# Layer 3's weight tiles taken by twos, in a four-layer graph network on one core

## The chip, the cores and the metric

The kernel runs on one core of one Trainium2 chip. The metric is the time on the device in microseconds, from start to end of one execution. The kernel before took 2709.49 us (median of three runs, 2709.22 to 2711.38).

## The reference, cut to what matters

There are 16 graphs of 1024 nodes with 256 features each, and an adjacency matrix of 1024 x 1024 whole numbers (0 or 1) for each. Four layers follow each other, each a layer norm, a relu and a graph layer that is added to x: two attention layers of one head, a layer of mean messages, and an attention layer of four heads with 64 features a head. The fourth is the one that is changed:

```python
h = einsum('bnd,hde->bhne', nodes_embed, W)            # H = 4 heads, 64 features each
weight = mask * (e_src[:, :, :, None] + e_dst[:, :, None, :])
weight = leaky_relu(weight, negative_slope=0.01)
weight = where(node_adj[:, None] == 0, NEG, weight)
attention = softmax(weight, axis=-1)
dst = einsum('bhij,bhje->bhie', attention, h) + bias
out = relu(dst) + h                                    # then a norm over each head's 64 features
```

(The reference sums over five kinds of edges; with an adjacency of zeros and ones only the first is there.)

## The kernel before

Each graph is a Python generator that records instructions, and each `yield` says by how many units the graph moves on in a list. The recorder always takes the graph with the lowest position, so the yields decide how the instructions of neighbouring graphs are mixed. Graphs start 120 units apart, and one is some 260 long: two or three are under way at a time. A scheduler then sets the final order on each engine; what is marked `later` keeps its place.

Layer 3 makes the unnormalised attention of one head in tiles `p` of 128 source nodes x 1024 target nodes on VectorE, and multiplies each tile at once on TensorE. A product takes 64 target nodes as its stationary side (`part`), so two of them, `c` = 0 and 1, use two halves of the array's columns. The outcome has 65 columns, 64 features and the sum for the softmax. Eight outcomes share one PSUM tile, `pss[g]`, four for each g. `start` is set on the first write to a PSUM tile alone.

```python
def layer3(b, xs, mask, norm, res):
    ...                                    # projection, exponentials, hb: features times exp, and exp
    yield 8
    for h in range(H):
        next_row = everywhere(d_row[h + 1], "row3") if h + 1 < H else None
        pss = [hd_ps.tile([P, HALF], F32, tag="hd", name="ps_o3") for _ in range(NHALF)]
        for j in range(NT):
            p = work.tile([P, N], F32, tag="p3", name="p3", bufs=3)
            nc.vector.scalar_tensor_tensor(p, row, q[:, j, h : h + 1], mask[:, j, :], op0=OP.max, op1=OP.mult)   # L887
            for i in range(NT):
                g, k = divmod(i, PER)
                for c in range(2):
                    part = slice(c * P // 2, (c + 1) * P // 2)
                    nc.tensor.matmul(                                                                            # L893
                        pss[g][part, k * HW : (k + 1) * HW], p[:, i * P : (i + 1) * P][:, part], hbv[:, j, h, :],
                        start=(j == 0 and k == 0), stop=(j == NT - 1 and k == PER - 1), skip_group_check=True,
                    )
            yield 1.4
        for g in range(NHALF):             # read out: L901, L902
            o = pss[g][:, : PER * HW].rearrange("p (k e) -> p k e", e=HW)
            rz = small.tile([P, PER], F32, tag="rz", name="rz")
            nc.vector.reciprocal(rz, o[:, :, HO])
            nc.vector.tensor_tensor(res[:, g * PER : (g + 1) * PER, h, :], o[:, :, :HO], ..., op=OP.mult)
        row = next_row
    return hs
```

The `hd` pool has two PSUM tiles, so a head can't begin until the head ahead of it is read out. Layer 1 has the same kind of tile, with products of full width: each of its first two row blocks gets its product as soon as a tile is there, the other six afterwards.

```python
def layer1(b, xs, mask, norm, after):
    ...
    (d_row,) = spread(column(hs[:, :, D + 1 : D + 2], 1), 1, (S - 1.0,), "l1")   # a transpose on TensorE (L672), ...
    row = everywhere(d_row, "row")                                             # ... then out to DRAM and back (DMA)
    yield 5
    for j in range(NT):
        p = weights("p1")                                                      # eight buffers
        nc.vector.scalar_tensor_tensor(p, row, q[:, j : j + 1], mask[:, j, :], op0=OP.max, op1=OP.mult)  # L793
        for i, ps in enumerate(early):
            product(ps, i, j)                                                  # L786, 128 x 257
        yield 1.3
    ...
```

The rest is only named here: projections (L659), transposes (L653), layer 0's products (L730), layer 2's (L844), and `tail`, the last norm of a graph.

Of the kernel before, what the change touches and what calls it, by code (L numbers as in the profile page):

```python
# [8 lines left out]
F32 = mybir.dt.float32  # L9
# [412 lines left out]
def tile_simple_stack(  # L422
# [22 lines left out]
    S, S3 = 0.2, 0.01  # L445
    W3 = D + 2 * H
    HW = HO + 1
    STEP = 1.3
    EARLY = 2

    const = ctx.enter_context(tc.tile_pool(name="const", bufs=1))
# [261 lines left out]
    def layer0(b, xs, m, norm, after):  # L713
        hs = new_hs()
        for n in range(NT):
            ps = project(norm, wx[0], n, D + 2)
            nc.scalar.activation(hs[:, n, : D + 2], ps[:, : D + 2], AF.Copy, scale=norm.rs[n])  # L717
            m.step()
            yield 1.2
        mask = m.bytes  # L720
        row_a, row_b = [everywhere(d, "row") for d in spread(column(hs[:, :, D : D + 1], 1), 1, (1.0, S), "l0")]
        q = small.tile([P, NT], F32, tag="q", name="q")
        nc.scalar.activation(q, hs[:, :, D + 1], AF.Exp, scale=1.0 - S)
        watch(b, 0, hs[:, :, D : D + 2])
        yield 5
        ps_ = []
        early = [at_ps.tile([P, HALF], F32, tag="at", name="ps_o0") for _ in range(EARLY)]

        def product(ps, i, j):
            m = nc.tensor.matmul(  # L730
                ps[:, :D], ps_[j][:, i * P : (i + 1) * P], hs[:, j, :D], start=(j == 0), stop=(j == NT - 1)
            )
            if i < EARLY and j < 7:
                later(m)

        for j in range(NT):
            if m.raws:
                m.step(2)
            p = weights("p0")
            nc.vector.scalar_tensor_tensor(p, row_a, q[:, j : j + 1], row_b, op0=OP.mult, op1=OP.max)  # L740
            z = small.tile([P, 2], F32, tag="z", name="z", bufs=8)
            nc.vector.scalar_tensor_tensor(p, p, 1.0, mask[:, j, :], op0=OP.mult, op1=OP.mult, accum_out=z[:, 0:1])
            nc.vector.reciprocal(z[:, 1:2], z[:, 0:1])
            nc.scalar.activation(hs[:, j, :D], hs[:, j, :D], AF.Copy, scale=z[:, 1:2])  # L744
            ps_.append(p)
            if b == 0:
                gates.append(p)
            for i, ps in enumerate(early):
                if j:
                    product(ps, i, j - 1)  # L750
            yield 2.6
        for i, ps in enumerate(early):
            product(ps, i, NT - 1)
        for i in range(NT):
            if i < EARLY:
                ps = early[i]
            else:
                ps = at_ps.tile([P, HALF], F32, tag="at", name="ps_o0")
                for j in range(NT):
                    product(ps, i, j)  # L760
            e = work.tile([P, D], F32, tag="e", name="e")
            nc.scalar.activation(e, ps[:, :D], AF.Exp)  # L762
            v = work.tile([P, D], F32, tag="v", name="v")
            nc.scalar.copy(v, ps[:, :D])  # L764
            residual(xs, i, v, after, e)
            yield 3.9


    def layer1(b, xs, mask, norm, after):
        hs = new_hs()  # L770
        for n in range(NT):
            ps = project(norm, wx[1], n, D + 2)
            nc.scalar.activation(hs[:, n, : D + 2], ps[:, : D + 2], AF.Copy, scale=norm.rs[n])
            yield 1.4
        (d_row,) = spread(column(hs[:, :, D + 1 : D + 2], 1), 1, (S - 1.0,), "l1")
        row = everywhere(d_row, "row")
        watch(b, 1, hs[:, :, D : D + 2])
        q = small.tile([P, NT], F32, tag="q", name="q")
        nc.scalar.activation(q, hs[:, :, D], AF.Exp, scale=1.0 - S)
        nc.scalar.activation(hs[:, :, D], hs[:, :, D], AF.Exp, scale=S)  # L780
        yield 5
        ps_ = []
        early = [at_ps.tile([P, HALF], F32, tag="at", name="ps_o1") for _ in range(EARLY)]

        def product(ps, i, j):
            nc.tensor.matmul(  # L786
                ps[:, : D + 1], ps_[j][:, i * P : (i + 1) * P], hs[:, j, : D + 1], start=(j == 0), stop=(j == NT - 1)
            )

        for j in range(NT):  # L790
            nc.scalar.activation(hs[:, j, :D], hs[:, j, :D], AF.Copy, scale=hs[:, j, D : D + 1])
            p = weights("p1")
            nc.vector.scalar_tensor_tensor(p, row, q[:, j : j + 1], mask[:, j, :], op0=OP.max, op1=OP.mult)  # L793
            ps_.append(p)
            for i, ps in enumerate(early):
                product(ps, i, j)
            yield 1.3
        for i in range(NT):
            if i < EARLY:
                ps = early[i]  # L800
            else:
                ps = at_ps.tile([P, HALF], F32, tag="at", name="ps_o1")
                for j in range(NT):
                    product(ps, i, j)
            k = b * NT + i
            z = shares[:, k : k + 1]
            nc.vector.reciprocal(z, ps[:, D : D + 1])  # L807
            e = work.tile([P, D], F32, tag="e", name="e")
            nc.scalar.activation(e, ps[:, :D], AF.Exp, scale=z)  # L809
            v = work.tile([P, D], F32, tag="v", name="v")  # L810
            nc.scalar.activation(v, ps[:, :D], AF.Copy, scale=z)
            residual(xs, i, v, after, e)
            yield 3.9


    def layer2(b, xs, norm, after):
# [12 lines left out]
        for n in range(NT):  # L829
            ps = project(norm, wx[2], n, 2 * D)  # L830
            rs = norm.rs[n]
            nc.scalar.activation(hi[:, n, :D], ps[:, :D], AF.Copy, scale=rs)  # L832
            rest = work.tile([P, D], F32, tag="e", name="rest")
            nc.scalar.activation(rest, ps[:, :D], AF.Copy, scale=rs)
            nc.scalar.activation(up[:, n, :D], ps[:, D:], AF.Copy, scale=rs)
            nc.vector.tensor_tensor(lo[:, n, :D], rest, hi[:, n, :D].bitcast(F32), op=OP.subtract)
            nc.vector.tensor_tensor(up[:, n, :D], up[:, n, :D], rows["bias2"], op=OP.add)
            yield 1.1
        for j in range(NT):
            g, jj = divmod(j * P, QUART)  # L840
            ps = hd_ps.tile([P, HALF], F32, tag="hd", name="ps_o2")
# [11 lines left out]
            nc.scalar.copy(edges[:, k : k + 1], ps[:, D : D + 1])  # L853
            nc.vector.tensor_tensor(v, v, up[:, j, :D], op=OP.add)
            residual(xs, j, v, after)
            yield 3.5


    def layer3(b, xs, mask, norm, res):
# [4 lines left out]
        for n in range(NT):  # L864
            ps = project(norm, wx[3], n, W3)
            nc.scalar.activation(hs[:, n, :], ps[:, :W3], AF.Copy, scale=norm.rs[n])
            if n % 2:
# [4 lines left out]
                bias = rows["bias3"].rearrange("p (h e) -> p h e", e=HO).unsqueeze(1).to_broadcast([P, 2, H, HO])  # L872
                nc.vector.tensor_tensor(t, hv, bias, op=OP.add)
                nc.vector.tensor_tensor(t, t, hbv[:, pair, :, HO:].to_broadcast([P, 2, H, HO]), op=OP.mult)
            yield 1.2
        d_row = spread(column(terms[:, :, :H], H), H, (S3 - 1.0,), "l3")
        row = everywhere(d_row[0], "row3")
        watch(b, 2, terms)
        q = small.tile([P, NT, H], F32, tag="q3", name="q3", bufs=2)
        nc.scalar.activation(q, terms[:, :, H:], AF.Exp, scale=1.0 - S3)  # L880
        yield 8
        for h in range(H):
            next_row = everywhere(d_row[h + 1], "row3") if h + 1 < H else None
            pss = [hd_ps.tile([P, HALF], F32, tag="hd", name="ps_o3") for _ in range(NHALF)]
            for j in range(NT):
                p = work.tile([P, N], F32, tag="p3", name="p3", bufs=3)
                nc.vector.scalar_tensor_tensor(p, row, q[:, j, h : h + 1], mask[:, j, :], op0=OP.max, op1=OP.mult)  # L887

                for i in range(NT):
                    g, k = divmod(i, PER)  # L890
                    for c in range(2):
                        part = slice(c * P // 2, (c + 1) * P // 2)
                        nc.tensor.matmul(  # L893
                            pss[g][part, k * HW : (k + 1) * HW], p[:, i * P : (i + 1) * P][:, part], hbv[:, j, h, :],
                            start=(j == 0 and k == 0), stop=(j == NT - 1 and k == PER - 1), skip_group_check=True,
                        )
                yield 1.4
            for g in range(NHALF):
                o = pss[g][:, : PER * HW].rearrange("p (k e) -> p k e", e=HW)
                rz = small.tile([P, PER], F32, tag="rz", name="rz")  # L900
# [48 lines left out]
    def graph(b):  # L949
# [3 lines left out]
        for g in range(NT // 2):  # L953
            norm.pair(xs, g)
            m.step()
            yield 2
        for layer, inputs in ((layer0, (m,)), (layer1, (m.bytes,)), (layer2, ())):
            yield 2
            norm.flip()
            after = Norm()  # L960
            yield from layer(b, xs, *inputs, norm, after)
            norm = after
        yield 2
        norm.flip()
        res = state.tile([P, NT, H, HO], F32, tag="res", name="res", bufs=1)
        hs = yield from layer3(b, xs, m.bytes, norm, res)
# [3 lines left out]

    def loads(b):
        loaded[b] = load_x(b)
        yield 50
        masks[b] = Mask(b)
        yield 0

# [2 lines left out]
    def more():  # L979

        weights01(1, w1, w1_t, a1, (1, 0))
        yield 20
        weights2()
        yield 10
        weights3()
        yield 0

# [1 line left out]
    next(loads_0)  # L989
    weights01(0, w0, w0_t, a0, (0, 1), wait=False)  # L990
    next(loads_0)
    queue = [(33, 0, more())] + [(b * APART, b, graph(b)) for b in range(B)] + [(b * APART - 60, b, loads(b)) for b in range(1, B)]
    while queue:
        queue.sort(key=lambda g: g[:2])
        at, b, g = queue.pop(0)
# [86 lines left out]
```

## Time and profile before

| what | before |
|---|---|
| median of three runs | 2709.49 us |
| span of the profiled run | 2701.4 us |
| instructions | 62281 |
| DMA traffic | 233.73 MB, 87 GB/s on average |
| granted TensorE clock | 0.978 of full speed |

TensorE's products have the name PE in the profile, its weight loads PEld, VectorE is DVE, ScalarE ACT, GpSimd POOL. A float32 product is two instructions each in the profile, so a layer-3 tile, which has 16 products, shows as 32. The page gives each engine's busy time, the span in 40 slices with a digit for the busy tenths, the DMA queues, the chain of work that ended last, and groups of equal instructions. A group's row reads: line, engine, operation, output and inputs, shapes, count, then busy us and mean ns of one, then the idle time just before them and what ended most of it. Matmuls overlap in a pipeline, so the time of one is read from start to start, and not from its duration.

### The profile page before, as it was taken

To read this page: it belongs to the slowest core of one execution; us is meant where nothing else is said; L and a number is where in the kernel's file an instruction comes from. 1 tells how busy PE (TensorE), PEld (TensorE's weight loads), DVE (VectorE), ACT (ScalarE), POOL (GpSimd) and SP (SyncE) were. 2 spreads that over 40 slices of the span, in tenths; PEclk is the share of its full clock that TensorE was granted. 3 is DMA by queue.
4 is the path that set the end of the run, shared out by engine and by line. 5 is a ranking of instruction groups with operands and counts; after the bars stand their busy time and mean duration, and the time that the engine had idled before them with its cause. 6 is when DMAs were issued, how large, how long until landed. Compare 5 with 4: busy or idle time off the path is not lost.

```text
span 2701.4 us, 62281 instructions
## 1 busy us (share of the span) xinstructions
PE 2504.5 (93%) x25682; PEld 2018.0 (75%) x25682; DVE 2021.2 (75%) x4069; ACT 1432.5 (53%) x4065; POOL 418.1 (15%) x390
## 2 busy tenths in 40 slices
PE   5899999999999999999999999999999999999985
PEld 4677787776777778687776877778787777877764
DVE  4357768687686977779677687887778777786868
ACT  4663755627455364654637546374653737546250
POOL 1010212102121030211102111020210202121021
PEclk7899999999999999999999999999999999999998
DMA  4431322424223242331413224242332413224121
GB/s 145 117 83 52 114 72 67 122 64 125 76 69 108 65 120 66 98 80 64 133 53 114 72 64 125 65 133 68 96 82 64 133 52 114 74 63 113 37 63 35
DMA packets 146073, 233.73 MB, mean 87 GB/s; under 512 B 9392, under 2 KB 94512, under 8 KB 145776
## 3 DMA queue, kind: packets, MB, share of 16 engines
q1 hardware_dynamic: 74608, 145.73, 16.7%
q0 software_dynamic: 71168, 83.89, 12.4%
q8 instruction: 205, 3.36, 0.5%
q14 instruction: 92, 0.75, 0.1%
HBM read 212.35 MB, written 17.24 MB: 85 GB/s over the span
## 4 chain that ended last, share of the span: by engine, by line
PE 50%; DMA 13%; issue 13%; DVE 13%; ACT 10%; POOL 1%; SPq 0%; DVEq 0%; POOLq 0%; ACTq 0%
PE ps_o L893 14%; PE ps_o L730 12%; PE ps_proj L659 9%; PE ps_o L786 9%; DMA raw<-in_adj_t 5%; PE ps_o L844 5%; DVE p L887 4%; DMA adj<-in_adj 4%; DMA row<-d_row 3%; PE pt_h L653 2%; ACT hn L631 2%; ACT mask L575 2%; ACT unread L635 1%; DMA d_row<-e_row 1%; DVE p L793 1%
## 5 line engine op out<-in xcount | busy, mean ns | idle before, releaser
L887 DVE SCALAR_TENSOR_TENSOR p<-row,q,mask 128x1024 f32<-128x1024 f32 x512 | 635.3, 1276 | 38.8 <-PE ps_o L893 30.0
L659 PE MATMUL ps_proj<-wx,ht 128*128 128x258 f32 (+2 forms) x2048 | 631.5, 444 | 19.4 <-ACT hs L717 12.8
L893 PEld LDWEIGHTS ps_o<-hb,p 128*64 128x64 f32 x16384 | 513.2, 139 | 126.1 <-issue 72.2
L893 PE MATMUL ps_o<-hb,p 128*64 128x65 f32 x16384 | 563.1, 225 | 16.2 <-DVE p L887 11.1
L786 PE MATMUL ps_o<-hs,p 128*128 128x257 f32 x2048 | 529.7, 398 | 50.0 <-DVE p L793 41.0
L730 PE MATMUL ps_o<-hs,p 128*128 128x256 f32 x2048 | 492.6, 387 | 14.5 <-ACT hs L744 14.0
L659 PEld LDWEIGHTS ps_proj<-wx,ht 128*128 128x128 f32 x2048 | 362.2, 190 | 186.7 <-issue 75.5
L786 PEld LDWEIGHTS ps_o<-hs,p 128*128 128x128 f32 x2048 | 372.1, 193 | 112.6 <-issue 48.5
L730 PEld LDWEIGHTS ps_o<-hs,p 128*128 128x128 f32 x2048 | 383.8, 193 | 70.7 <-ACT hs L744 15.3
L592 POOL TENSOR_SCALAR rs<-mv 128x4 f32<-128x4 f32 (+1 forms) x112 | 56.9, 508 | 1600.3 <-ACT unread L635 1584.7
L631 ACT ACTIVATE hn<-xs,shift 128x256 f32<-128x256 f32 x512 | 236.1, 501 | 115.7 <-DVE shift L627 112.9
L707 DVE SCALAR_TENSOR_TENSOR xs<-e,xs 128x256 f32<-128x256 f32 x256 | 108.2, 423 | 236.8 <-ACT e L762 204.3
L593 POOL TENSOR_TENSOR rs<-rs,neg_half 128x4 f32<-128x4 f32 (+2 forms) x144 | 259.7, 1806 | 10.7
L809 ACT ACTIVATE e<-ps_o,shares 128x256 f32<-128x256 f32 x128 | 59.7, 466 | 349.7 <-DVE shares L807 345.5
L575 ACT ACTIVATE mask<-raw 128x512 uint8<-128x512 int32 x256 | 160.5, 630 | 133.8 <-DMA raw<-in_adj_t 114.7
L844 PE MATMUL ps_o<-hi,adj 128*128 128x258 f32 x1024 | 184.9, 308 | 35.5 <-ACT hi L832 23.7
L653 PE MATMUL pt_h<-ident,hn 128*128 128x128 f32 x1024 | 177.5, 283 | 16.5 <-ACT hn L631 16.2
L635 ACT ACTIVATE unread<-xs,shift 128x256 bf16<-128x256 f32 x384 | 190.7, 497 | 0.6
L844 PEld LDWEIGHTS ps_o<-hi,adj 128*128 128x128 f32 x1024 | 144.3, 192 | 60.7 <-ACT hi L832 29.7
L740 DVE SCALAR_TENSOR_TENSOR p<-row,q 128x1024 f32<-128x1024 f32 x128 | 161.1, 1269 | 30.5 <-DMA row<-d_row 30.5
L654 ACT COPY ht<-pt_h 128x512 f32<-128x512 f32 x256 | 147.2, 588 | 67.3 <-PE pt_h L653 66.8
L708 DVE SCALAR_TENSOR_TENSOR xs<-v,xs 128x256 f32<-128x256 f32 x384 | 161.6, 421 | 26.2 <-ACT v L764 9.7
(101 smaller groups left out, 2644.4 us busy)
## 6 DMA issues: line engine op xcount, KB each, us to landing
raw<-in_adj_t SPq DMA_DIRECT2D x256, 256.0 KB
adj<-in_adj POOLq DMA_DIRECT2D x64, 1024.0 KB, 5.8
row<-d_row SPq DMA_DIRECT2D x112, 512.0 KB
xs<-in_x POOLq DMA_DIRECT2D x32, 512.0 KB, 6.3
out<-res SPq DMA_DIRECT2D x32, 512.0 KB
wx<-in_w SPq DMA_DIRECT2D x3, 256.0 KB
d_row<-e_row SPq DMA_DIRECT2D x48, 4.0 KB
wts<-in_w_t SPq DMA_DIRECT2D x2, 256.0 KB
```

The costliest lines, as they stand in the source:

```text
L575: nc.scalar.activation(self.bytes[:, n, g * HALF : (g + 1) * HALF], raw, AF.Square, accum_out=squares[:, k : k + 1])
L593: nc.gpsimd.tensor_tensor(rs[:, :n], rs[:, :n], neg_half[:, :n], op=OP.pow)
L631: nc.scalar.activation(hn, xs[:, 2 * g + k, :], AF.Relu, bias=shift[:, k : k + 1])
L635: nc.scalar.activation(unread, xs[:, 2 * g + k, :], AF.Square, bias=shift[:, k : k + 1], accum_out=self.var[:, 2 * g + k : 2 * g + k + 1])
L653: nc.tensor.transpose(pt[:, c, k * P : (k + 1) * P], hn[:, c * P : (c + 1) * P], ident)
L659: nc.tensor.matmul(ps[:, :width], norm.ht[:, c, n * P : (n + 1) * P], w[:, c, :width], start=(c == 0), stop=(c == DC - 1))
L708: nc.vector.scalar_tensor_tensor(x, v, 0.0, x, op0=OP.max, op1=OP.add, accum_out=after.sums[:, i % 2 : i % 2 + 1])
L730: m = nc.tensor.matmul(ps[:, :D], ps_[j][:, i * P : (i + 1) * P], hs[:, j, :D], start=(j == 0), stop=(j == NT - 1))
L786: nc.tensor.matmul(ps[:, : D + 1], ps_[j][:, i * P : (i + 1) * P], hs[:, j, : D + 1], start=(j == 0), stop=(j == NT - 1))
L844: nc.tensor.matmul(ps[:, : D + 2], adj_n[g][:, i, jj : jj + P], h[:, i, : D + 2], start=(h is hi and i == 0), stop=(h is lo and i == NT - 1),)
L887: nc.vector.scalar_tensor_tensor(p, row, q[:, j, h : h + 1], mask[:, j, :], op0=OP.max, op1=OP.mult)
L893: nc.tensor.matmul(pss[g][part, k * HW : (k + 1) * HW], p[:, i * P : (i + 1) * P][:, part], hbv[:, j, h, :], start=(j == 0 and k == 0), st ...
```

## The change

Layer 3 makes two tiles first and then multiplies both in one run of 32 products. The run begins with the two first products of the *second* tile, one for each PSUM tile, so that its only wait, for the second tile, stands at its head, and goes on with all of the first tile and the rest of the second. `start` and `stop` move with that order. The aim is that TensorE changes less often between these products and others, and that nothing stops it within a run. Three buffers serve the tiles, as before.

All steps of the list are set anew for it. No other instruction is added or taken away.

```diff
-    STEP = 1.3
+    STEP = 1.6                      # tail
 (layer 0)
-            yield 1.2
+            yield 0.9
-        yield 5
+        yield 4.8
 (layer 1)
-            yield 3.9
+            yield 3.74
 (layer 2)
-            yield 1.1
+            yield 1.14
-            yield 3.5
+            yield 3.22
 (layer 3)
-            yield 1.2
+            yield 1.15
-        yield 8
+        yield 9.44
...
-            for j in range(NT):
-                p = work.tile([P, N], F32, tag="p3", name="p3", bufs=3)
-                nc.vector.scalar_tensor_tensor(p, row, q[:, j, h : h + 1], mask[:, j, :], op0=OP.max, op1=OP.mult)
-
-                for i in range(NT):
+            for j in range(0, NT, 2):
+                ps_ = []
+                for jj in range(j, j + 2):
+                    p = work.tile([P, N], F32, tag="p3", name="p3", bufs=3)
+                    nc.vector.scalar_tensor_tensor(p, row, q[:, jj, h : h + 1], mask[:, jj, :], op0=OP.max, op1=OP.mult)
+                    ps_.append(p)
+
+                runs = [(1, 0), (1, PER)] + [(0, i) for i in range(NT)] + [(1, i) for i in range(NT) if i % PER]
+                for t, i in runs:
                     g, k = divmod(i, PER)
                     for c in range(2):
                         part = slice(c * P // 2, (c + 1) * P // 2)
                         nc.tensor.matmul(
-                            pss[g][part, k * HW : (k + 1) * HW], p[:, i * P : (i + 1) * P][:, part], hbv[:, j, h, :],
-                            start=(j == 0 and k == 0), stop=(j == NT - 1 and k == PER - 1), skip_group_check=True,
+                            pss[g][part, k * HW : (k + 1) * HW], ps_[t][:, i * P : (i + 1) * P][:, part], hbv[:, j + t, h, :],
+                            start=(j == 0 and t == 1 and k == 0), stop=(j == NT - 2 and t == 1 and k == PER - 1),
+                            skip_group_check=True,
                         )
-                yield 1.4
+                yield 2.8
...
 (graph: between layers, before layer 3)
-            yield 2
+            yield 2.36
-        yield 2
+        yield 1.92
 (loads: x first, the first mask tiles later)
-        yield 50
+        yield 30.0
 (more: the weights of layers 1 to 3, for the first graph)
-        yield 20
+        yield 21.6
...
-    queue = [(33, 0, more())] + ... + [(b * APART - 60, b, loads(b)) for b in range(1, B)]
+    queue = [(32, 0, more())] + ... + [(b * APART - 80, b, loads(b)) for b in range(1, B)]
```

With both, x is fetched 80 units ahead of its graph's start (60 before), and the first mask tiles 50 ahead (10 before).

More of the change, by code (lines that the diff above doesn't have):

```diff
@@ L780, in layer1 @@
         nc.scalar.activation(hs[:, :, D], hs[:, :, D], AF.Exp, scale=S)
-        yield 5
+        yield 5.0
         ps_ = []
@@ L955, in graph @@
             m.step()
-            yield 2
+            yield 2.0
         for layer, inputs in ((layer0, (m,)), (layer1, (m.bytes,)), (layer2, ())):
-            yield 2
+            yield 2.36
             norm.flip()
@@ L962, in graph @@
             norm = after
-        yield 2
+        yield 1.92
         norm.flip()
@@ L981, in more @@
         weights01(1, w1, w1_t, a1, (1, 0))
-        yield 20
+        yield 21.6
         weights2()
-        yield 10
+        yield 10.0
         weights3()
@@ L991, in tile_simple_stack @@
     next(loads_0)
-    queue = [(33, 0, more())] + [(b * APART, b, graph(b)) for b in range(B)] + [(b * APART - 60, b, loads(b)) for b in range(1, B)]
+    queue = [(32, 0, more())] + [(b * APART, b, graph(b)) for b in range(B)] + [(b * APART - 80, b, loads(b)) for b in range(1, B)]
     while queue:
```

## The prediction

> **What bounds the kernel now.** I read the page from the top: engine shares, the 40 slices, the chain of waits, the groups.
>
> ```profile
> PE 2504.5 (93%) x25682; PEld 2018.0 (75%) x25682; DVE 2021.2 (75%) x4069; ACT 1432.5 (53%) x4065; POOL 418.1 (15%) x390
> ...
> PE   5899999999999999999999999999999999999985
> ...
> PE 50%; DMA 13%; issue 13%; DVE 13%; ACT 10%; POOL 1%; SPq 0%; DVEq 0%; POOLq 0%; ACTq 0%
> ```
>
> TensorE (PE) is the bound: busy 93% of 2701.4 us, below nine tenths only in the first two and last two slices, and half of the chain that ended last is PE. The idle 197 us divide roughly so: slices of 67.5 us at 5, 8, 8 and 5 tenths give about 34 + 13 + 13 + 34 = 94 us at the ends, so about 100 us in the middle, some 6 us for each of the 16 graphs. Next, the rows of the stage that is changed:
>
> ```profile
> L887 DVE SCALAR_TENSOR_TENSOR p<-row,q,mask 128x1024 f32<-128x1024 f32 x512 | 635.3, 1276 | 38.8 <-PE ps_o L893 30.0
> ...
> L893 PEld LDWEIGHTS ps_o<-hb,p 128*64 128x64 f32 x16384 | 513.2, 139 | 126.1 <-issue 72.2
> L893 PE MATMUL ps_o<-hb,p 128*64 128x65 f32 x16384 | 563.1, 225 | 16.2 <-DVE p L887 11.1
> ```
>
> VectorE (DVE) makes 512 weight tiles of 1.2 to 1.28 us each; TensorE multiplies each by 32 instructions on a 128*64 division of the array. PE waits for them almost nowhere (11.1 us in all), while DVE waits 30.0 us for PE to release a tile: DVE runs ahead as far as three buffers allow. So the case for the change isn't a wait that is printed; it is the switching between 128*64 and 128*128 instructions. Start times of a stretch of the timeline, PE alone, show it:
>
> ```profile
> 1418.09 1.15 PE L893 MATMUL ps_o<-hb,p 128*64 128x65 f32 x32
> 1419.17 0.70 PE L786 MATMUL ps_o<-hs,p 128*128 128x257 f32 x2
> 1419.80 2.09 PE L893 MATMUL ps_o<-hb,p 128*64 128x65 f32 x64
> 1421.82 0.70 PE L786 MATMUL ps_o<-hs,p 128*128 128x257 f32 x2
> 1422.36 0.60 PE L653 MATMUL pt_h<-ident,hn 128*128 128x128 f32 x4
> 1422.89 3.02 PE L893 MATMUL ps_o<-hb,p 128*64 128x65 f32 x96
> 1425.84 3.73 PE L786 MATMUL ps_o<-hs,p 128*128 128x257 f32 x16
> 1429.50 1.15 PE L893 MATMUL ps_o<-hb,p 128*64 128x65 f32 x32
> 1430.58 3.73 PE L786 MATMUL ps_o<-hs,p 128*128 128x257 f32 x16
> 1434.15 0.72 PE L653 MATMUL pt_h<-ident,hn 128*128 128x128 f32 x4
> ```
>
> From start to next start a run of 32 takes 1.08 us, of 64 takes 2.02, of 96 takes 2.95. Each further 32 costs 0.935 us (29.2 ns an instruction), so 0.145 us of each run belong to leaving it. The entrance costs too: 16 instructions of L786 take 3.66 us ahead of an L893 run (1425.84 to 1429.50) and 3.57 us ahead of transposes (1430.58 to 1434.15), 0.09 us more. A visit to the 128*64 division thus costs about 0.24 us beside its products.
>
> The second thing to see is where PE really stands in layer 3: at the start of the next graph's layer 1, and on DVE. First PE, then DVE, then shares of both in three stretches (us, PE, PEld, DVE, ACT, POOL, clock, DMA, GB/s).
>
> ```profile
> 1389.01 4.89 PE L893 MATMUL ps_o<-hb,p 128*64 128x65 f32 x160
> 1396.43 2.30 PE L786 MATMUL ps_o<-hs,p 128*128 128x257 f32 x8 [2.53 <-DVE p L793]
> ```
>
> ```profile
> 1388.93 6.16 DVE L887 SCALAR_TENSOR_TENSOR p<-row,q,mask 128x1024 f32<-128x1024 f32 x5 [0.34 <-PE ps_o L893]
> 1395.00 2.48 DVE L793 SCALAR_TENSOR_TENSOR p<-row,q,mask 128x1024 f32<-128x1024 f32 x2
> ```
>
> ```profile
> 1370.00:1392.00 22.00, 21.77 (x483) 18.23 (x483) 19.69 (x25) 9.13 (x25) 3.18 (x2) 1.00 0.10 29
> 1392.00:1412.00 20.00, 17.38 (x292) 13.64 (x288) 20.00 (x23) 1.23 (x3) 0.00 (x0) 1.00 0.29 92
> 1412.00:1434.00 22.00, 22.00 (x371) 18.57 (x370) 18.50 (x46) 10.03 (x29) 0.00 (x0) 1.00 0.20 63
> ```
>
> Between 1392 and 1412 DVE hasn't a free moment (20.00 of 20) and PE has (17.38): there DVE sets the pace, and PE waits 2.53 us for the first layer-1 tile. Over the 64 us DVE is busy 58.2 us, PE 61.2. The stage is nearly balanced, so PE time saved in it is worth less than its face.
>
> **What the Trainium skill says.** "TensorEngine Tiling (Array Packing)", section "Key Properties", says that a change of tiling mode, and not merely of tile, drains TensorE. The trace agrees: the 0.145 and 0.09 us above are paid at changes of mode only. "Perfetto Trace Analysis", section "Optimization Strategy", says that a gap which recurs on the engine that should be saturated can mean too few buffers for the next tile. The kernel before shows that on the other side (DVE waits 30.0 us for PE to release); the change works with the same three buffers.
>
> **The change part by part.**
>
> *Switches.* In the instruction order of the two programs, TensorE enters the 128*64 division 331 times before and 256 times after (about 21 and 16 times a graph). It isn't halved, because the old order had 90 runs of more than one tile already, and the new one splits some pairs into runs of 4, 5 and 6 products among layer 1's. 75 x 0.24 us = 18 us saved, all on PE.
>
> *Waits inside runs.* A long run before could stop at a tile's semaphore; a pair now waits once, at its head. The run of 160 above lasts 4.89 us where 160 x 29.2 ns is 4.67 and its last instruction's own time fills most of the rest, so little is to be had: 3 us.
>
> *The rhythm of pairs.* New cost. A pair needs both tiles, and with three buffers only one tile of the next pair can be made before this pair gives one back. The order of products gives back the first tile after 8 + 32 of 64 instructions, 40 x 29.2 ns = 1.17 us after the pair starts; the missing tile then takes 1.28 us, and the hand-overs some 0.1 us (estimate). Pairs can't start closer than about 2.55 us, against 1.87 us of products plus whatever other work stands between. The new order puts 0.87 to 1.74 us (two to four projections, or L786 products) between most pairs, which covers it, but nothing between three in a row ahead of layer 1 (there 2 us, which mostly fall on the 2.53 us PE waits now), and too little at the change of heads, where a pair needs two fresh tiles and both accumulators read out: 0.3 to 1.4 us. I set 1.2 us a graph: 16 x 1.2 = 19 us lost.
>
> *The steps.* The list of stages is set to finer numbers (layer 0's projections 0.9 for 1.2, layer 3's start 9.44 for 8, layer 2's products 3.22 for 3.5, the tail 1.6 for 1.3), the input of a graph is fetched 20 units earlier and its first mask tiles 40 earlier. No instruction is added. What it can win is the 100 us of PE idle in the middle and the 94 us at the ends. DVE waits 49.2 us for x, ScalarE 114.7 us for the raw mask tiles (list of waits), and both stand partly in the way of layer 2's operands. Numbers of this kind are found by trial, so I expect them to be no worse than before; I give them a seventh of the idle 197 us: 28 us. This is chosen, not derived.
>
> Sum: -18 - 3 + 19 - 28 = -30 us, 2709.5 to 2680 us.
>
> **Rivals.**
> 1. Pairs starve. If the lead of three single tiles was what hid the jitter of DVE, each of the 16 pairs can lose up to 0.7 us (2.55 less 1.87): 11 us a graph, 180 us at worst. For: DVE is full in 1392 to 1412. Against: between most pairs there is other work. A third of it, with the switches saved and nothing from the steps, makes 2750 us.
> 2. Nothing comes of it. DVE is the bound where layers 3 and 1 overlap, so the PE time saved turns into a longer wait for L793: 2700 to 2710 us.
> 3. The steps do the work. If they close half of the middle's idle and let the last graph start sooner, 50 to 70 us on top of the switches: 2630 us. For: about 20 numbers were set again together. Against: the order around layer 1's start and layer 2's start, where PE waits most, looks much like the old one (layer 1's first product again stands behind about 80 of layer 3's).
>
> **Range and chances.** Middle 2680 us. The low end, 2637, is rival 3 nearly in full; the high end, 2726, is the switches saved and a fifth of rival 1 without help from the steps. 2% faster is 2655 us: it needs the steps to bring twice what I gave them, 0.2. 2% slower is 2764 us: rival 1 at nearly half, 0.05. Within: 0.75.
>
> **What would show it.** TensorE's busy time for the layer-3 products falls from 563 us by about the exit part of the switches, 75 x 0.145 = 11 us, and the time of L786 and L659 by the entrance part. A pair is a run of 64 with 2.02 us to the next start. PE's waits for layer-3 tiles grow from 11.1 us to 20 to 40 us: that is the rhythm. DVE's waits for PE's release grow beyond 30.0 us. PE's wait for layer 1's first tile stays at 2 to 4 us a graph. If the span falls by more than 55 us, the slices at the ends or the waits around layer 2 must have changed; if it grows, the pairs' waits are over 60 us. I am wrong if the switch count doesn't show in PE's busy time, or if the steps move the time by more than 60 us either way.

## The result and the profile after

The changed kernel takes 2666.51 us (median of four runs, 2663.33 to 2669.82), against 2709.35 us (median of four runs): the ratio is 0.9844, with a 95% interval of 0.9827 to 0.9861. It is 1.6% faster. The profiled run spans 2664.8 us, 36.6 us less than before. The page of the changed kernel, parts 1, 2 and 4 (L889 and L898 are now the lines of layer 3's tiles and products):

```profile
PE 2462.6 (92%) x25682; PEld 2011.5 (75%) x25682; DVE 2028.6 (76%) x4069; ACT 1427.7 (54%) x4065; POOL 391.5 (15%) x390
...
PE   5899999999999999999999999999999999999974
...
PE 47%; DVE 19%; ACT 14%; DMA 10%; issue 10%; POOL 1%; SPq 0%; DVEq 0%; ACTq 0%; POOLq 0%
```

TensorE's busy time fell by 41.9 us and its idle time (span less busy) rose from 196.9 to 202.2 us. VectorE's part in the chain that ended last rose from 13% to 19%. So TensorE's instructions, the same in number, take less time, but it doesn't stand idle less. Part 5 of the same page, layer 3's rows:

```profile
L889 DVE SCALAR_TENSOR_TENSOR p<-row,q,mask 128x1024 f32<-128x1024 f32 x512 | 642.8, 1280 | 77.3 <-PE ps_o L898 69.3
L898 PEld LDWEIGHTS ps_o<-hb,p 128*64 128x64 f32 x16384 | 508.3, 138 | 168.0 <-DVE p L889 107.8
...
L898 PE MATMUL ps_o<-hb,p 128*64 128x65 f32 x16384 | 549.6, 224 | 78.3 <-DVE p L889 52.8
```

The products are busy 13.5 us less than before, as fewer switches would make them. But the idle time ahead of them grew from 16.2 to 78.3 us, and VectorE's wait for a released tile from 30.0 to 69.3 us: the two engines now wait for each other (the second of these waits comes with the steps, as single tiles will show). The timeline of TensorE at the start of the next graph's layer 1 shows how (in brackets: idle before, and what ended it):

```profile
1359.28 2.09 PE L898 MATMUL ps_o<-hb,p 128*64 128x65 f32 x64
1361.29 0.27 PE L672 MATMUL ps_col<-ident,col 128*8 128x128 f32 x1
1362.05 2.09 PE L898 MATMUL ps_o<-hb,p 128*64 128x65 f32 x64 [0.48 <-DVE p L889]
1365.47 2.18 PE L898 MATMUL ps_o<-hb,p 128*64 128x65 f32 x64 [1.33 <-DVE res L908]
1368.33 1.26 PE L898 MATMUL ps_o<-hb,p 128*64 128x65 f32 x34 [0.68 <-DVE p L889]
1369.62 1.11 PE L786 MATMUL ps_o<-hs,p 128*128 128x257 f32 x4
```

Pairs with no more than one transpose (L672) between them start 2.77 us (1359.28 to 1362.05) and 2.86 us (1365.47 to 1368.33) apart, though a run of 64 takes 2.0 us to the next start; at the change of heads, where the accumulators have to be read out first, it is 3.42. Layer 1's first product, which waited 2.53 us before, waits no more: the wait now lies in the pieces ahead of it.

The rest of the fall in busy time stands outside layer 3. Layer 1's products (L786) take 509.7 us where they took 529.7, and the projections (L659) 619.8 where they took 631.5, with the same instructions. The granted clock bears on this. Its mean is 0.978 in the profiled run before and 0.985 after (0.984 to 0.985 in the four runs of the changed kernel, 0.968 to 0.981 in all those of the kernel before). Between 200 and 2550 us the kernel before has 13 stretches of 3.41 us each at half clock, the changed kernel one. In both, each of them began within 5 us of the start of a TensorE gap of some 1.8 us or more; 8 of the 13 gaps before stood ahead of layer 1's products, 5 ahead of layer 2's (nine gaps as long were followed by no such stretch). One of the 13, first TensorE's timeline, then the gap and the stretch after it (the columns are those of the windows in the prediction, the clock third from the end):

```profile
1558.58 3.25 PE L786 MATMUL ps_o<-hs,p 128*128 128x257 f32 x8 [2.52 <-DVE p L793]
```

```profile
1556.10:1559.29 3.19, 0.71 (x3) 0.68 (x4) 3.19 (x3) 0.00 (x0) 0.00 (x0) 1.00 0.90 273
1559.29:1562.71 3.42, 3.42 (x24) 2.14 (x24) 3.42 (x7) 0.00 (x0) 0.00 (x0) 0.50 0.34 116
```

The eight products took 3.25 us here and 2.30 us after the gap at 1396.43, which the prediction shows and which no half clock followed. TensorE's idle time between 200 and 2550 us is the same in both kernels, 108.8 and 108.6 us, but of gaps over 1.5 us there were 24 (61.1 us) and are 2 (3.4 us). An estimate from these sums: of the 41.9 us of busy time, about 20 are half-clock stretches that are gone (12 of 3.41 us, at half their length), and about 18 are 75 fewer switches at 0.24 us. No run holds the clock fixed, so this split is argued and not shown by an experiment. The experiments take the two halves of the change apart.

### The profile page after: what moved, and what is told of

The parts are those of the page before. It is cut to its first block, busy times and chain, and to the rows that moved or that the text cites. A ratio compares the mean times of both kernels' runs of the same rounds, so it can differ in the third digit from the quotient of the medians.

```text
span 2664.8 us, 62272 instructions
## 1 busy us (share of the span) xinstructions
PE 2462.6 (92%) x25682; PEld 2011.5 (75%) x25682; DVE 2028.6 (76%) x4069; ACT 1427.7 (54%) x4065; POOL 391.5 (15%) x390
## 4 chain that ended last, share of the span: by engine, by line
PE 47%; DVE 19%; ACT 14%; DMA 10%; issue 10%; POOL 1%; SPq 0%; DVEq 0%; ACTq 0%; POOLq 0%
PE ps_proj L659 14%; PE ps_o L730 11%; PE ps_o L898 11%; DVE p L889 9%; PE ps_o L844 5%; DVE p L793 5%; ACT hn L631 4%; DMA raw<-in_adj_t 4%; PE ps_o L786 3%; DMA adj<-in_adj 3%; ACT mask L575 2%; PE pt_h L653 2%; ACT unread L635 2%; DMA row<-d_row 2%; ACT e L809 1%
## 5 line engine op out<-in xcount | busy, mean ns | idle before, releaser
L889 DVE SCALAR_TENSOR_TENSOR p<-row,q,mask 128x1024 f32<-128x1024 f32 x512 | 642.8, 1280 | 77.3 <-PE ps_o L898 69.3
L898 PEld LDWEIGHTS ps_o<-hb,p 128*64 128x64 f32 x16384 | 508.3, 138 | 168.0 <-DVE p L889 107.8
L659 PE MATMUL ps_proj<-wx,ht 128*128 128x258 f32 (+2 forms) x2048 | 619.8, 443 | 11.6 <-ACT hs L717 7.1
L898 PE MATMUL ps_o<-hb,p 128*64 128x65 f32 x16384 | 549.6, 224 | 78.3 <-DVE p L889 52.8
L786 PE MATMUL ps_o<-hs,p 128*128 128x257 f32 x2048 | 509.7, 391 | 22.2 <-ACT v L811 13.1
L659 PEld LDWEIGHTS ps_proj<-wx,ht 128*128 128x128 f32 x2048 | 365.6, 190 | 174.5 <-issue 76.6
L786 PEld LDWEIGHTS ps_o<-hs,p 128*128 128x128 f32 x2048 | 368.6, 191 | 82.1 <-ACT v L811 22.1
L592 POOL TENSOR_SCALAR rs<-mv 128x4 f32<-128x4 f32 (+1 forms) x112 | 46.3, 414 | 1660.8 <-ACT unread L635 1593.4
L593 POOL TENSOR_TENSOR rs<-rs,neg_half 128x4 f32<-128x4 f32 (+2 forms) x144 | 251.2, 1752 | 9.4
L844 PE MATMUL ps_o<-lo,adj 128*128 128x258 f32 x1024 | 184.3, 303 | 0.0
L844 PE MATMUL ps_o<-hi,adj 128*128 128x258 f32 x1024 | 166.9, 300 | 12.3 <-DMA adj<-in_adj 11.9
L653 PEld LDWEIGHTS pt_h<-ident,hn 128*128 128x128 f32 x1024 | 123.0, 142 | 67.3 <-ACT hn L631 42.7
```

The source lines that it names most:

```text
L593: nc.gpsimd.tensor_tensor(rs[:, :n], rs[:, :n], neg_half[:, :n], op=OP.pow)
L653: nc.tensor.transpose(pt[:, c, k * P : (k + 1) * P], hn[:, c * P : (c + 1) * P], ident)
L659: nc.tensor.matmul(ps[:, :width], norm.ht[:, c, n * P : (n + 1) * P], w[:, c, :width], start=(c == 0), stop=(c == DC - 1))
L786: nc.tensor.matmul(ps[:, : D + 1], ps_[j][:, i * P : (i + 1) * P], hs[:, j, : D + 1], start=(j == 0), stop=(j == NT - 1))
L844: nc.tensor.matmul(ps[:, : D + 2], adj_n[g][:, i, jj : jj + P], h[:, i, : D + 2], start=(h is hi and i == 0), stop=(h is lo and i == NT - 1),)
L889: nc.vector.scalar_tensor_tensor(p, row, q[:, jj, h : h + 1], mask[:, jj, :], op0=OP.max, op1=OP.mult)
```

## The experiments

All ratios are to the kernel before on the same chip, with 95% intervals. "Entries" is the count of visits to the 128*64 products in TensorE's order, given in brackets with old and with new steps.

| layer 3's tiles | old steps | new steps |
|---|---|---|
| single (331; 316 entries) | 1 | 0.9782 (0.9726 to 0.9838) |
| pairs, second tile's start at the head (211; 256) | 1.0062 (1.0046 to 1.0078) | 0.9844 (0.9827 to 0.9861), the changed kernel |
| pairs, first tile first (286; 241) | 0.9889 (0.9867 to 0.9912) | 0.9721 (0.9666 to 0.9776) |

**The pairs alone, with old steps** (the pair's loop, and one step of 2.8):

```diff
-            for j in range(NT):  ...  yield 1.4
+            for j in range(0, NT, 2):  ...  yield 2.8      # all other steps as before
```

> The pairs alone, with every step of the list as before (the two single steps of 1.4 become one of 2.8). TensorE enters the layer-3 products 211 times here (331 before, 256 in the changed kernel). Theory A (the steps made the gain, the pairs give back in waits what they save in switches): 2695 to 2725 us, TensorE idle ahead of the layer-3 products over 60 us (16.2 before). Theory B (the pairs made the gain): 2665 to 2685 us.

Measured: 2727.03 us, ratio 1.0062. The idle time ahead of the layer-3 products is 112.2 us, 103.6 of them for a tile, though the entries fell to 211. Layer 1's first tile, by contrast, costs 7.3 us of waits where it cost 41.0. The pairs as written lose more than they save; theory B falls.

**The new steps alone, with single tiles:**

```diff
-            for j in range(0, NT, 2):  ...  yield 2.8
+            for j in range(NT):  ...  yield 1.4            # all other steps as in the changed kernel
```

> The new steps alone, layer 3 by single tiles as before, 316 entries into its products. Theory A: 2655 to 2685 us, as fast as the changed kernel or faster, with the waits around layer 2 short as there. Theory B: 2700 to 2725 us. If both this and the pairs alone stay near 2709 us, the two only work together.

Measured: 2653.91 us, ratio 0.9782, 12 us faster than the changed kernel's order in the run beside it (2666.27, with the old loads, below). So the steps without the pairs bring all the gain of the change and more. VectorE's wait for a released tile is 68.4 us here, and the wait for the read-out at the change of heads 23.0 (2.6 before): neither needs the pairs.

**Pairs in plain order, with the new steps:**

```diff
-                runs = [(1, 0), (1, PER)] + [(0, i) for i in range(NT)] + [(1, i) for i in range(NT) if i % PER]
+                runs = [(0, i) for i in range(NT)] + [(1, i) for i in range(NT)]
-                            start=(j == 0 and t == 1 and k == 0), ...
+                            start=(j == 0 and t == 0 and k == 0), ...
```

> The changed kernel, but a pair's products in plain order: all of the first tile, then all of the second; start and stop moved to match. The first tile goes back after 32 instructions of 64 and not 40 (0.23 us sooner), and a run can begin when the first tile is there; its second wait stands in the middle. If the waits for the second tile at the head of a run are what costs (theory A), 5 to 20 us faster than the changed kernel's 2666.5 us: 2646 to 2662 us. If one unbroken run is what pays (theory B), slower: 2672 to 2695 us. The scheduler splits some runs here (241 entries).

Measured: 2638.03 us, ratio 0.9721, 28 us below the changed order on the same chip, more than I expected. This is the fastest kernel of the study. The same place in its timeline:

```profile
1350.71 2.09 PE L898 MATMUL ps_o<-hb,p 128*64 128x65 f32 x64
1352.72 0.27 PE L672 MATMUL ps_col<-ident,col 128*8 128x128 f32 x1
1352.93 2.09 PE L898 MATMUL ps_o<-hb,p 128*64 128x65 f32 x64
1356.28 4.62 PE L898 MATMUL ps_o<-hb,p 128*64 128x65 f32 x146 [1.27 <-DVE res L908]
1361.39 1.10 PE L786 MATMUL ps_o<-hs,p 128*128 128x257 f32 x4 [0.49 <-DVE p L793]
```

The second pair follows 2.22 us after the first, with the transpose between, where the changed order took 2.77: it needn't wait for its second tile. The read-out at the change of heads stays (1.27 us). Over the whole run the idle time ahead of the layer-3 products is 39.6 us and not 78.3, of which tiles are 11.0 and not 52.8. The plain order has both: fewer entries than single tiles (241 for 316) and hardly more waits (39.6 us for 37.3). It is 15.9 us faster than single tiles with the same steps, where 75 entries fewer at 0.24 us come to 18 (estimate).

**The same plain order with the old steps**, which separates order from steps:

> Pairs in plain order (first tile, then second) with every old step: 286 entries into the layer-3 products. With the second tile's start at the head the same steps took 2727.0 us, with single tiles 2709. If that order is what the pairs lose by, 2690 to 2712 us here, and TensorE's idle time ahead of layer-3 products below 35 us; if pairs as such starve, over 2718 us.

Measured: 2676.09 us, ratio 0.9889, better than the range I gave, with 42.5 us of idle time ahead of the products, over the 35 I gave, but 10.0 of them for tiles (103.6 with the other order). It is 32.8 us faster than single tiles with the same steps. So pairs as such don't starve; the start of the second tile at the head of the run does it, with either set of steps.

**A fourth buffer.** It needs memory. In both kernels of this comparison the rows of layer 3's bias, gamma and beta are left out, layer 2's bias row stands in for them, and three small tiles have one buffer less:

```diff
+        rows["bias3"] = rows["gamma3"] = rows["beta3"] = rows["bias2"]      # both
-  tag="e_row" bufs=2; tag="col" bufs=2; name="m3" bufs=2                    # both
+  tag="e_row" bufs=1; tag="col" bufs=1; name="m3" bufs=1
-  tag="p3" bufs=3                                                           # lean_pairs4 alone
+  tag="p3" bufs=4
```

> Control for the fourth buffer: the changed kernel with memory made free. The rows of layer 3's bias, gamma and beta aren't loaded and layer 2's bias row stands in for them (so the output lacks gamma and the shift), and three small tiles have one buffer less. The order of layer 3's products is that of the changed kernel, 256 entries. 2655 to 2675 us: no theory expects more than 10 us from 2666.5.

> The same with four buffers for layer 3's tiles instead of three, so that both tiles of the next pair can be made during this one. If the shortage of tiles is what the pairs pay (theory A), TensorE's idle time ahead of layer-3 products falls from 78 us to below 45, DVE's wait for release from 69 us to below 25, and the time is 10 to 25 us below its control. If the wait is only DVE's total work (rival), within 5 us of its control.

Measured: 2696.83 us for the control (0.9955, 0.9941 to 0.9969) and 2680.89 us with the fourth buffer (0.9893, 0.9876 to 0.9909). The control missed its range: what was done to free the memory, meant to be harmless, cost 30 us; which part of it did stays open. Against that control the fourth buffer brings 16 us. The products' rows, control first, then four buffers:

```profile
L898 PE MATMUL ps_o<-hb,p 128*64 128x65 f32 x16384 | 550.3, 224 | 78.3 <-DVE p L889 52.9
```

```profile
L898 PE MATMUL ps_o<-hb,p 128*64 128x65 f32 x16384 | 540.0, 224 | 53.6 <-DVE res L908 28.9
```

The idle time falls by 24.7 us: waits for tiles fall by 28.4 (52.9 to 24.5 in the list of waits) and those for the read-out grow by 4.9 (24.0 to 28.9). VectorE's wait for release falls from 69.7 to 46.0. It points the way theory A says, though less far than I expected (45 and 25): a fourth buffer halves the waits for tiles, the plain order with three buffers removes four fifths. One reserve: the scheduler also made fewer entries with four buffers (241 for 256), so some of the 16 us is switching, about 4 by 0.24 us each (estimate).

**Which of the steps?** First the loads of x and masks, put back in the changed kernel:

```diff
-        yield 30.0          # in loads
+        yield 50
-        (b * APART - 80, b, loads(b))
+        (b * APART - 60, b, loads(b))
```

> The changed kernel with the loads of x and of the first mask tiles where they were (60 and 10 units ahead of a graph instead of 80 and 50). If the earlier loads made the gain, by ending DVE's waits for x (49.2 us before) and ScalarE's for raw mask tiles (114.7 us), 2685 to 2710 us. If the mixing of the graphs' instructions made it, no more than 5 us from 2666.5 us.

Measured: 2666.27 us, ratio 0.982 (0.9765 to 0.9875). The changed kernel took 2666.51: no gain of these loads shows.

Then groups of steps, each alone on single tiles:

```diff
 s_layer0:    1.2 -> 0.9, 5 -> 4.8
 s_layers12:  3.9 -> 3.74, 1.1 -> 1.14, 3.5 -> 3.22, gaps 2 -> 2.36 and 2 -> 1.92
 s_layer3:    1.2 -> 1.15, 8 -> 9.44, tail 1.3 -> 1.6
```

> Single tiles, old steps, but layer 0's two new ones (projection 0.9 for 1.2, 4.8 for 5). All the new steps together with single tiles took 2653.9 us, 58 less than before. If the mixing of layer 0 with the layer 2 ahead of it is the seat of the gain, 2670 to 2690 us; otherwise 2700 to 2715 us.

> Single tiles, old steps, but the new ones of layers 1 and 2 and between the layers (3.74, 1.14, 3.22, gaps 2.36 and 1.92). Layer 2's products are the place with the longest TensorE gaps that shrank (5.2 us a graph before, 3.2 after); if these steps do it, 2670 to 2690 us; otherwise 2700 to 2715 us.

> Single tiles, old steps, but those of layer 3 and the tail (projection 1.15, 9.44 for 8 ahead of the heads, tail 1.6 for 1.3). They move layer 3's tiles later against the next graph's layer 1, where TensorE waits 2.5 us a graph for its first tile. If that is the seat of the gain, 2670 to 2690 us; otherwise 2700 to 2715 us.

Measured: 2740.91 us (1.0108, 1.0055 to 1.0161), 2720.64 us (1.003, 1.0016 to 1.0044) and 2717.64 us (1.0023, 1.001 to 1.0036). Each of the three missed: none gains, all three lose a little. So I left out one group at a time:

> Single tiles with the new steps of layers 0, 1 and 2, but layer 3, the tail and the loads as before. Each group alone was no faster (2741, 2721, 2718 us); all together 2654 us. With those of layers 1 and 2 alone, TensorE's waits for layer 1's first tile and for layer 2's operands fell, and a new wait came: layer 2's projection for ScalarE's third eviction (75 us on the weight loads, 43 on the products). If layer 0's earlier projection (theory L0) takes that wait away, 2655 to 2680 us here and over 2700 without it. If it is layer 3's later tail (theory L3), over 2700 us here.

> Single tiles with the new steps of layers 1, 2, 3 and the tail, but layer 0 and the loads as before. Theory L0: over 2700 us, with layer 2's projection still waiting 60 us and more for ScalarE. Theory L3: 2655 to 2680 us. If both of these stay over 2690 us, all three groups are needed.

Measured: without layer 3 and the tail 2699.88 us (0.9963, 0.9952 to 0.9974); without layer 0 2643.37 us (0.9755, 0.9733 to 0.9777), all the gain (with layer 0's it was 0.9782, and the intervals overlap), though every load is where it was before. Theory L0 falls; L3 fits, though both times are just below what it gave (over 2700, 2655 to 2680). The steps of layers 1 and 2 and those of layer 3 and the tail together make the gain, and neither group does alone. Why not? The timeline of s_layers12, all engines, cut to one stop of layer 2's projection:

```profile
1470.28 0.75 POOL L545 DMA_DIRECT2D xs<-in_x  x1
...
1475.47 0.75 DVE L623 BATCH_NORM_STATS2 st<-xs 128x6 f32<-128x256 f32 x2 [4.42 <-DMA xs<-in_x]
1476.05 0.63 ACT L575 ACTIVATE mask<-raw 128x512 uint8<-128x512 int32 x1 [2.60 <-DMA raw<-in_adj_t]
...
1476.68 0.46 ACT L832 ACTIVATE hi<-ps_proj,rs 128x256 fp32r<-128x256 f32 x1
...
1477.39 0.47 ACT L835 ACTIVATE up<-ps_proj,rs 128x256 f32<-128x256 f32 x1
...
1477.92 3.93 PE L659 MATMUL ps_proj<-wx,ht 128*128 128x512 f32 x5 [2.43 <-ACT up L835]
```

ScalarE stands at a mask tile of the *next* graph whose data hasn't come (2.60 us), VectorE at that graph's x (4.42 us, fetched 5.2 us ahead), and this graph's evictions L832 and L835 stand behind the mask tile. TensorE waits at the end of that line. From the lists of waits (total us, times, longest), first s_layers12, then s_layer3, then both groups together (s_no_layer0):

```profile
DVE st L623 <- DMA xs<-in_x: 77.7, 15, 7.5
PE ps_proj L659 <- ACT up L835: 42.7, 31, 4.0
PE ps_o L786 <- DVE p L793: 14.0, 16, 7.5
```

```profile
PE ps_o L844 <- DMA adj<-in_adj: 39.4, 16, 4.4
PE ps_o L786 <- DVE p L793: 38.1, 15, 2.7
```

```profile
DVE st L623 <- DMA xs<-in_x: 10.1, 2, 7.3
PE ps_o L786 <- DVE p L793: 8.6, 15, 1.8
PE ps_o L844 <- DMA adj<-in_adj: 6.7, 13, 1.4
PE ps_proj L659 <- ACT up L835: 2.8, 15, 0.2
```

The new steps of layers 1 and 2 do remove a wait of before (layer 1's first tile, 41.0 us, is 14.0), but the projection's wait for ScalarE grows from 5.6 to 42.7 us. Those of layer 3 alone keep that one at 2.1 us and leave layer 1's first tile at 38.1; the idle time ahead of layer 2's products (L844, from `hi`) has another name, the adjacency, but hardly another size, 39.4 us where 35.5 were. With both, none of the four waits listed is over 10.1 us.

The waits are not all of it. TensorE's idle time (span less busy), and its time at half clock between 200 and 2550 us, from the profiled runs:

| run | span | idle | at half clock |
|---|---|---|---|
| before | 2701.4 | 196.9 | 44.4 |
| s_layer0 | 2737.1 | 223.0 | 61.4 |
| s_layers12 | 2728.2 | 200.3 | 54.6 |
| s_layer3 | 2718.4 | 199.1 | 81.9 |
| s_no_layer3 | 2702.2 | 191.1 | 13.7 |
| s_no_layer0 | 2644.4 | 155.2 | 0 |
| singles_new_steps | 2650.3 | 161.0 | 3.4 |
| changed kernel | 2664.8 | 202.2 | 3.4 |

s_layer3 is 17.0 us longer than the kernel before with 2.2 us more idle time: 37.5 us more at half clock, which cost half their length, cover the difference (estimate: 19 us). s_layer0 loses by both; in s_layers12, whose profiled run was the slowest of its twenty, the two cover only a part. I read it so: the steps fix which graph's instruction stands in front on each engine when a transfer is late, and a long gap of TensorE that comes of it can cost a second time, in the clock. That the waits and the time at half clock differ so is shown; the reading isn't, nor which single step decides it.

## Why the prediction was right, and where it wasn't

The predicted 2680 us and its range hold 2666.5, and the direction was right. But two terms of the sum were too small and partly offset each other, and the granted clock isn't in the sum at all: that 2680 came so near is in part luck.

- *Bound by TensorE, layer 3 nearly balanced with VectorE.* Right. In the middle stretch of the overlap VectorE is still full (columns: us, PE, PEld, DVE, ACT, POOL, clock, DMA, GB/s):

```profile
1361.00:1381.00 20.00, 16.66 (x299) 13.49 (x293) 19.56 (x20) 2.95 (x8) 0.00 (x0) 1.00 0.16 54
```

- *Switches, -18 us.* Right in mechanism; the products' busy time fell by 13.5 us where 11 were given for the exits. (Of runs longer than one tile the trace before has 106, where I gave 90; the 331 entries are right.) The sign that I gave for the entrances can't be read: L786 and L659 fell by 31.7 us together, where 75 entrances at 0.09 us make 7, since the clock changed as well.
- *Rhythm of pairs, +19 us.* Right in mechanism, mis-sized. Starts are 2.77 to 2.86 us apart where I had 2.55, and the waits for tiles came to 52.8 us where I said 20 to 40. With the new steps pairs cost 12 us net against single tiles (2666.27 and 2653.91 on one chip); with 60 entries saved at 0.24 us put back, the rhythm took about 27 us (estimate). I had let the filling work cover most pairs. What I had foreseen at the change of heads came, but not from the pairs: the read-out's waits are 23.9 us (2.6 before), 23.0 with single tiles and the new steps, 7.9 with pairs and the old ones. In the same way VectorE's wait for release grew as forecast, but does so with single tiles too (68.4), so that sign didn't tell.
- *Steps, -28 us.* The seat of the gain, and mis-sized: 58 us alone (2711.8 to 2653.91). I called it chosen and not derived, took it as a share of the idle time, and gave the loads of x and masks as a part of it; these had none. With single tiles the idle time did fall, by 35.9 us; in the changed kernel the pairs took that back (202.2 us where 196.9 were), and what is left of the steps there is, by the sums above, mostly the clock.
- *Layer 1's first tile, 2 to 4 us a graph.* Wrong: it went from 41.0 us in all to 8.7. The wait moved forward into the runs of layer 3, as shorter gaps. That wasn't for nothing, since 8 of the 13 half-clock stretches before had followed gaps ahead of these products.
- *Rivals.* The first (pairs starve) was at work, and alone it made the kernel slower. The second (a longer wait for L793) didn't come. The third (steps do the work) came to the size it gave, but not on top of the pairs' gain: in place of it.

## What to carry to other kernels

Ask of a change that makes runs longer what must be there before a run starts and when its first buffer comes back: a single wait at the head of a pair cost more than the pairs saved in switches, and the same pair with its first tile first kept the savings without the wait. When steps or priorities are tuned along with a change, run the new steps on the old code: here they alone gave more than the whole change. And don't judge such steps one by one, since a wait removed in one place came back in another until two groups were moved together. Read the granted clock beside busy and idle time: here equal idle time, cut into shorter gaps, went with 12 half-clock stretches fewer.

## What the runs showed of the hardware

The drain at a change of tiling mode, which the Trainium skill has in "TensorEngine Tiling (Array Packing)", section "Key Properties", without a figure, has one here, worked out from the starts in the prediction: about 0.09 us to enter the 128*64 mode and 0.145 us to leave it, beside 29.2 ns for each instruction in it. Between 200 and 2550 us half clock came in stretches of 3.41 us, or of two such, in every run but s_no_layer0, which had none; in the kernel before each followed a TensorE gap of 1.87 to 4.46 us. I hadn't expected that three small tiles, `e_row`, `col` and `m3`, with one buffer less each, together with the rows left out, would cost 30 us.
